# Gathering one more tile in the same batch by plain DMAs, with a Newton root and row copies on VectorE

## The chip, the cores and the metric

One core of a Trainium2 chip runs the whole program. Its engines work side by side, each through a queue of its own: TensorE (PE, with its weight loads as PEld), VectorE (DVE), ScalarE (ACT), GpSimd (POOL) and SyncE (SP, which only issues transfers). The metric is the time of one execution on the device in microseconds (us), taken as the median over runs. One further execution was recorded by the profiler, and all durations below come from it.

## The reference

It is a recommendation network. For a batch of B = 16384 users there are L = 200 history items each; every item id is looked up in a table of 64-number rows, and the rows are weighted by an attention network and summed:

```python
h = i_emb[hist]                       # (200, 16384, 64)
feat = concat([h, it, h - it, h * it])
a = dice(feat @ au_W1 + au_b1, au_alpha, axis=1)
w = a @ au_W2 + au_b2
cur = sum(w * h, axis=0)
# dice(x): p = sigmoid((x - mean) * rsqrt(var + 1e-8)); x * (p + alpha * (1 - p))
```

The mean and variance inside `dice` are taken over the batch, for each history position l by itself. So the attention weights of position l need the statistics of all 16384 rows of l. After the 200 positions a small network of three layers (the head) turns user, item, category and `cur` into two numbers for each user.

## The kernel before

A **tile** is 128 rows of the table, a **step** is 16 tiles (1024 columns of TensorE work once transposed), and a history position l is 8 steps, c = 0 to 7, so that step k = 8l + c. There are 1600 steps. The first 180 positions run in a hardware loop of 45 positions per turn, the last 20 and the head are written out.

Every step is put into the engines' queues by `step` (L383), in the order of its lines, which is kept as written. Step k fetches its own tiles, turns those of step k−1 (transposes on VectorE, matmuls on TensorE), moves the hidden layer of step k−2 out of PSUM, and applies the attention weights to step k−9, whose position has its statistics by then:

- `fetch` (L319): GpSimd issues one indirect DMA for each tile (L123), into one of 5 buffers `rows`. A buffer is free again when the transposes of step k−5 have read it.
- `hidden` (L338): ScalarE copies the PSUM tile `px` to `xs` with the bias added (L339).
- at the end of a position (when k−2 is the last step of l) `measure` and `moments` (L341, L363): VectorE takes the batch statistics of l. `scale_and_shift` (L167) forms 1/sqrt(var + eps) from them: a Sqrt on ScalarE (L170), then a reciprocal and one multiplication on VectorE (L171, L172). Sqrt and Sigmoid need different tables on ScalarE, so each such root brings two table loads with it.
- `gate` (L326): ScalarE takes the sigmoid of `xs` of step k−9 (L328), with scale and shift of its position.
- `place` (L346) and `rows_by_address` (L279): see below.
- `turn` (L354): four transposes on VectorE (L156), then matmuls into `ph` and `px`; `product` (L359): VectorE forms `hm` from `ph` (L360), TensorE adds its part to `px`; `weights` and `weigh` (L330, L334): VectorE forms `y` (L331), TensorE forms `wb`, VectorE multiplies it and adds it to `curT` (L335, L336).

**Tiles by address.** Not all 128 tiles of a position come by indirect DMA. In some steps (c in `SIDES`, that is 1, 3, 4, 5, 6, 7) the 16th tile is fetched row by row, with one plain DMA of 256 bytes for each of its 128 rows. Step c = 5 does so only where l is a multiple of `EACH` = 3, so a position has 6 such tiles in one case of three and 5 otherwise. I call them six-tile and five-tile positions. Their rows are shared evenly over the 8 steps of the position: 96 rows in each step of a six-tile position, 80 in a five-tile one. Half of them are issued by SyncE and half by ScalarE. The addresses are ids times 256, which VectorE scales (L148); an engine reads up to 20 of them into registers with one load (L293) and then issues one DMA for each (L301). The rows land in one of three buffers `side`; each landing counts up a semaphore. In step k+1 `place` waits on ScalarE until all 128 rows have landed, clears the semaphore (`await_rows`, L309), and copies the tile to `rows` on ScalarE (L352). The last tile (c = 7) has its last rows issued in step 7 itself and is placed in step 8, before the next rows are issued.

Where c = 5 is not by address, SyncE loads 128 more ids for it (`sidx`, L142), and GpSimd gathers the 16th tile as the others.

Of the kernel before, what the change touches and what calls it, by code (L numbers as in the profile page):

```python
# [25 lines left out]
SIDES = (1, 3, 4, 5, 6, 7)  # L26
SOMETIMES = 5
EACH = 3
LOAD = 20
ROW = 4 * D  # L30
U8 = mybir.dt.uint8

# [2 lines left out]
def din_kernel(  # L35
# [130 lines left out]

    def scale_and_shift(mean, var, rstd, shift):  # L167
        n = mean.shape[0]
        std = small.tile([P, 1], F32, tag="std", name="std")
        nc.scalar.activation(std[:n], var, AF.Sqrt, bias=eps[:n])  # L170
        nc.vector.reciprocal(rstd, std[:n])  # L171
        nc.vector.scalar_tensor_tensor(shift, mean, -1.0, rstd, ALU.mult, ALU.mult)  # L172

    eps = make("eps", P, 1)
    blk_h = make("blk_h", P, P)
    blk_i = make("blk_i", P, P)
    blk_m = make("blk_m", P, P)
# [9 lines left out]
    halves = [(0, S), (S, A - S)]  # L187

    def attention_weights():
        nc.vector.memset(eps, EPS)  # L190
# [82 lines left out]
    def tiles_by_address(l):  # L273

        round_, i = divmod(l, EACH)
        first = round_ * (EACH * (NS - 1) + 1) + i * (NS - 1) + (i > 0)
        return first, [j for j, c in enumerate(SIDES) if has_side(l * ND + c)]

    def rows_by_address(k):  # L279
        l, s = divmod(k, ND)  # L280
        first, tiles = tiles_by_address(l)
        n = len(tiles) * P // ND // 2
        loads = -(-n // LOAD)
        for i, (engine, issue) in enumerate(
            ((mybir.EngineType.SP, nc.sync), (mybir.EngineType.Activation, nc.scalar))
        ):
            r0, end = (2 * s + i) * n, (2 * s + i + 1) * n
            while r0 < end:
                many = min(end - r0, -(-n // loads))
                at0 = tiles[r0 // P] * P + r0 % P  # L290
                while tiles[(r0 + many - 1) // P] * P + (r0 + many - 1) % P != at0 + many - 1:
                    many -= 1
                _, at = nc.values_load_multi_w_load_instructions(  # L293
                    addr[l % 3][:, at0 : at0 + many],
                    engines=(engine,), min_val=0, max_val=ROW * (V - 1),
                    skip_runtime_bounds_check_because="the DMA checks the address against the table",
                )
                for r, a in enumerate(at, r0):
                    m, p = first + r // P, r % P
                    key = keys.setdefault(m, f"rows{next(serial)}")  # L300
                    dma = issue.dma_start(  # L301
                        side[m % 3].bitcast(U8)[p : p + 1],
                        flat[ds(a, ROW)].rearrange("(o d) -> o d", o=1),
                    ).then_inc(landed[m % 3], 16)
# [78 lines left out]
    def step(k, last=None):  # L383

        def has(j):
            return last is None or j <= last

        ends = (k - 2) % ND == ND - 1
        if has(k):
            fetch(k)  # L390
        if has(k - 2):
            hidden(k - 2)
            if ends:
                measure(k - 2)
                moments((k - 2) // ND)
        if has(k - LAG):
            gate(k - LAG)
        if has(k - 1):
            place(k - 1)
        if has(k):  # L400
            rows_by_address(k)
        if has(k - 1):
            turn(k - 1)
        if has(k - 2) and not ends:
            measure(k - 2)
        if has(k - 1):
            product(k - 1)
        if has(k - LAG):
            weights(k - LAG)
            weigh(k - LAG)  # L410

    def steps(l0, n, end):
        for k in range(n * ND):
            l, c = divmod(k, ND)
            if c == 0 and l + 1 < end:
                load_hist_ids((l + 1) % IDX, l0 + l + 1)
                if (l + 1) % EACH:
# [183 lines left out]
```

## Time and profile before

| | |
|---|---|
| median of 13 runs | 31360.91 us (31251.99 to 31371.98) |
| the profiled execution | 31316.35 us, span 31314.6 us |
| busy: PE / DVE / ACT / POOL | 66% / 48% / 14% / 75% of the span |
| indirect DMAs on GpSimd | 24917, of which 24400 + 133 for the history |
| row DMAs, SyncE and ScalarE | 68288 each |
| granted TensorE clock | 0.805 |

The 13 runs fall into two groups, three near 31252 us and ten near 31360 us; the profiled one lies between them. Busy times count only the work of an engine: the time that ScalarE's queue spends on issuing DMAs, on loads of registers and on waits is not in its 14%. The queue's own rows are marked ACTq and SPq.

### The profile page before, as it was taken

Reading aid. Unit: us, or ns where it says so; the run is one execution under the profiler, and the core shown is the slowest. Engines: PE = TensorE matmul, PEld = TensorE weight load, DVE = VectorE, ACT = ScalarE, POOL = GpSimd, SP = SyncE. Lnnn points to the kernel's source line nnn. Section 1 sums busy time; section 2 is a strip of 40 time slices with the busy share of each in tenths; the row PEclk is TensorE's granted clock in tenths of the full one; section 3 lists DMA queues with packets and bytes.
Section 4 is the critical chain, followed back from the end, with each engine's and each line's share of the span. In section 5 each row is a group of like instructions: output and inputs, shape, how many; then the busy total and the mean of one; then the engine's idle time right before and its main releaser. Section 6 shows DMA issues by size and latency. Waiting matters only on the chain. (4 is left out here: it accounts for less than half of the span.)

```text
span 31314.6 us, 423966 instructions
## 1 busy us (share of the span) xinstructions
PE 20710.0 (66%) x38856; PEld 8498.5 (27%) x38856; DVE 15125.9 (48%) x18955; ACT 4403.8 (14%) x4941; POOL 23586.2 (75%) x24922
## 2 busy tenths in 40 slices
PE   5666666666666666666666666666666666666666
PEld 2222222222222222222222222222222222222222
DVE  4444444444444444444444444444444444444444
ACT  1111111111111111111111111111111111111111
POOL 7777777777777777777777777777777777777776
PEclk7877888887887788888878778888888888878887
DMA  1111111111111111111111111111111111111111
GB/s 29 29 29 29 29 29 29 29 29 29 29 29 29 29 29 29 29 29 29 29 29 29 29 29 29 29 29 29 29 29 29 29 29 29 29 29 29 29 29 24
DMA packets 1130924, 894.71 MB, mean 29 GB/s; under 512 B 729024, under 2 KB 729024, under 8 KB 1127896
## 3 DMA queue, kind: packets, MB, share of 16 engines
q0 software_dynamic: 797344, 818.07, 14.9%
q1 hardware_dynamic: 193112, 31.56, 0.6%
q10 hardware_dynamic: 137440, 17.76, 0.4%
q14 instruction: 2722, 22.30, 0.2%
q8 instruction: 306, 5.01, 0.1%
HBM read 865.10 MB, written 0.13 MB: 28 GB/s over the span
## 5 line engine op out<-in xcount | busy, mean ns | idle before, releaser
L123 POOL DMA_INDIRECT rows<-in_L_rec_i_emb,idx x24400 | 23096.4, 947 | 7472.5 <-issue 7231.1
L161 PE MATMUL ph<-hT,unit 128*128 128x512 f32 x6404 | 5899.2, 1069 | 10403.2 <-DVE hT L156 10401.2
L335 DVE SCALAR_TENSOR_TENSOR wb<-wb,au_bias,hT 128x1024 f32<-128x1024 f32 x1609 | 2080.0, 1293 | 10854.3 <-PE wb L161 10854.3
L156 DVE STREAM_TRANSPOSE hT<-rows 64x512 f32<-64x512 f32 x6404 | 4514.7, 705 | 2687.6 <-ACT rows L352 1797.0
L339 ACT ACTIVATE xs<-px,au_bias 128x1024 f32<-128x1024 f32 x1602 | 1785.1, 1114 | 25635.9 <-issue 11312.0
L161 PEld LDWEIGHTS ph<-hT,unit 128*128 128x128 f32 x6404 | 1727.5, 303 | 13432.7 <-DVE hT L156 13261.7
L161 PE MATMUL px<-hT,blk_h 128*128 128x512 f32 x6404 | 4111.1, 730 | 0.1
L161 PE MATMUL px<-itT,blk_i 128*128 128x512 f32 x6404 | 3342.4, 604 | 0.0
L161 PE MATMUL wb<-y,blk_p 128*128 128x512 f32 x6436 | 3295.2, 594 | 33.3 <-DVE y L331 33.3
L161 PE MATMUL wb<-xs,blk_x 128*128 128x512 f32 x6436 | 3293.2, 593 | 5.3 <-DVE curT L336 5.3
L161 PE MATMUL px<-hm,blk_m 128*128 128x512 f32 x6408 | 3013.0, 592 | 40.7 <-DVE hm L434 40.7
L360 DVE TENSOR_TENSOR hm<-ph,itT 128x1024 f32<-128x1024 f32 x1601 | 1961.1, 1225 | 1908.1 <-PE ph L161 1906.3
L161 PEld LDWEIGHTS px<-hT,blk_h 128*128 128x128 f32 x6404 | 1645.0, 257 | 2411.8 <-issue 2405.0
L344 DVE BATCH_NORM_STATS2 st<-xs 128x6 f32<-128x512 f32 x3204 | 2061.0, 685 | 231.0 <-ACT xs L339 186.0
L336 DVE TENSOR_TENSOR curT<-wb,curT 128x1024 f32<-128x1024 f32 x1609 | 1970.2, 1225 | 54.8
L331 DVE TENSOR_TENSOR y<-pg,xs 128x1024 f32<-128x1024 f32 x1609 | 1954.7, 1215 | 2.3 <-ACT pg L328 2.2
L161 PEld LDWEIGHTS px<-itT,blk_i 128*128 128x128 f32 x6404 | 1394.3, 218 | 2026.4 <-issue 2026.4
L328 ACT ACTIVATE pg<-xs,sh,rs 128x1024 f32<-128x1024 f32 x1609 | 1934.3, 1202 | 25.1 <-DVE y L331 20.1
L161 PEld LDWEIGHTS wb<-y,blk_p 128*128 128x128 f32 x6436 | 1224.9, 190 | 1578.6 <-issue 1539.6
L161 PEld LDWEIGHTS px<-hm,blk_m 128*128 128x128 f32 x6408 | 1217.9, 190 | 1573.4 <-issue 1532.7
L161 PEld LDWEIGHTS wb<-xs,blk_x 128*128 128x128 f32 x6436 | 1223.9, 190 | 1550.9 <-issue 1540.7
L352 ACT COPY rows<-side 128x64 f32<-128x64 f32 x1068 | 249.0, 233 | 315.5 <-DMA side<-in_L_rec_i_emb 179.8
(155 smaller groups left out, 2188.6 us busy)
## 6 DMA issues: line engine op xcount, KB each, us to landing
side<-in_L_rec_i_emb SPq DMA_DIRECT2D x68288, 0.2 KB
side<-in_L_rec_i_emb ACTq DMA_DIRECT2D x68288, 0.2 KB
rows<-in_L_rec_i_emb,idx POOLq DMA_INDIRECT x24400
idx<-in_r_hist SPq DMA_DIRECT2D x200, 61.0 KB
addrs<-in_r_hist SPq DMA_DIRECT2D x200, 3.0 KB
sidx<-in_r_hist SPq DMA_DIRECT2D x133, 0.5 KB
rows<-in_L_rec_i_emb,sidx POOLq DMA_INDIRECT x133
rows<-in_L_rec_i_emb,ids POOLq DMA_INDIRECT x128
```

Of the source, the lines that this page charges most:

```text
L123: nc.gpsimd.indirect_dma_start(out=dst[:, n, :], out_offset=None, in_=table, in_offset=bass.IndirectOffsetOnAxis(ap=ids, axis=0),)
L156: nc.vector.transpose(by_tile(dst[ts(e, D)], i), of[ts(i, D), :, ts(e, S)])
L161: nc.tensor.matmul(dst[:, ts(i, CH)], lhsT, rhs[:, ts(i, CH)], start=(first and j == 0), stop=(last and j == len(pairs) - 1), skip_group_c ...
L328: nc.scalar.activation(pg, xs[k % XR], AF.Sigmoid, bias=shifts[i], scale=rstds[i])
L331: nc.vector.tensor_mul(y, pg, xs[k % XR])
L335: nc.vector.scalar_tensor_tensor(wb, wb, au_bias2, hT[k % LAG], ALU.add, ALU.mult)
L336: nc.vector.tensor_add(curT[k % ND], wb, curT[k % ND])
L339: nc.scalar.activation(xs[k % XR], px, AF.Identity, bias=au_bias)
L344: nc.vector.bn_stats(stats[l % 3][:, 2 * c + i, :], xs[k % XR][:, ts(i, CH)])
L352: nc.scalar.copy(rows[k % ROWS][:, TD - 1], side[m % 3])
L360: nc.vector.tensor_mul(hm, ph, itT[k % ND])
```

## The change

It has four parts.

1. `MOST` = 2: step c = 5 takes its 16th tile by address where l % 3 is 0 or 1, no longer only where it is 0. So two positions of three are six-tile ones.
2. `scale_and_shift` uses no Sqrt. VectorE finds 1/sqrt(v) itself: a first guess by integer arithmetic on the bits, then three Newton steps, 12 small instructions in place of Sqrt and reciprocal.
3. `place` runs on VectorE: it waits there for the rows, clears the semaphore there, and copies the tile.
4. The rows of ScalarE are issued earlier in the step: one run of them (up to 20) between `hidden` and `gate`, the rest after `gate`. SyncE's are issued as before.

```diff
+MOST = 2
 def scale_and_shift(mean, var, rstd, shift):
-        std = small.tile([P, 1], F32, tag="std", name="std")
-        nc.scalar.activation(std[:n], var, AF.Sqrt, bias=eps[:n])
-        nc.vector.reciprocal(rstd, std[:n])
+        nc.vector.tensor_scalar_add(v, var, EPS)
+        nc.vector.tensor_single_scalar(h.bitcast(I32), v.bitcast(I32), 1, ALU.logical_shift_right)
+        nc.vector.tensor_scalar(
+            rstd.bitcast(I32), h.bitcast(I32), -1.0, float(0x5F375A00), ALU.mult, ALU.add
+        )
+        for _ in range(3):
+            nc.vector.scalar_tensor_tensor(h, rstd, v, rstd, ALU.mult, ALU.mult)
+            nc.vector.tensor_scalar(h, h, -0.5, 1.5, ALU.mult, ALU.add)
+            nc.vector.tensor_mul(rstd, rstd, h)
         nc.vector.scalar_tensor_tensor(shift, mean, -1.0, rstd, ALU.mult, ALU.mult)
...
+    def shares(k):
+        l, s = divmod(k, ND)
+        n = len(tiles_by_address(l)[1]) * P // ND
+        many = round(n * SPLIT)
+        runs = []
+        for r0, end in ((s * n, s * n + many), (s * n + many, (s + 1) * n)):
+            loads = -(-(end - r0) // LOAD)
+            at = [r0 + (end - r0) * i // loads for i in range(loads + 1)]
+            runs.append(list(zip(at, at[1:])))
+        return runs
...
     def await_rows(m):
         if m in keys:
-            fence = nc.scalar.wait_ge(landed[m % 3], 16 * P)
+            fence = nc.vector.wait_ge(landed[m % 3], 16 * P)
             tc.declare_fence(fence.ins, group=keys.pop(m))
-            nc.scalar.sem_clear(landed[m % 3])
+            nc.vector.sem_clear(landed[m % 3])
     def has_side(k):
-        return c in SIDES and (c != SOMETIMES or l % EACH == 0)
+        return c in SIDES and (c != SOMETIMES or l % EACH < MOST)
...
             await_rows(m)
-            nc.scalar.copy(rows[k % ROWS][:, TD - 1], side[m % 3])
+            nc.vector.tensor_copy(rows[k % ROWS][:, TD - 1], side[m % 3])
...
+        if has(k):
+            sync, scalar = shares(k)
+            ask(k, 0, sync)
+            ask(k, 1, scalar[:1])
         if has(k - LAG):
             gate(k - LAG)
+        if has(k):
+            ask(k, 1, scalar[1:])
         if has(k - 1):
             place(k - 1)
-        if has(k):
-            rows_by_address(k)
-        if has(k - 1):
             turn(k - 1)
```

`ask` issues one engine's runs as `rows_by_address` did, with one register load for each run of up to 20 rows (`SPLIT` = 0.5, so the halves are as before). The ids of `sidx` are loaded only where c = 5 is not by address.

More of the change, by code (lines that the diff above doesn't have):

```diff
@@ L28 @@
 EACH = 3
+MOST = 2
 LOAD = 20
+SPLIT = 0.5
 ROW = 4 * D
@@ L168, in scale_and_shift @@
         n = mean.shape[0]
-        std = small.tile([P, 1], F32, tag="std", name="std")
-        nc.scalar.activation(std[:n], var, AF.Sqrt, bias=eps[:n])
-        nc.vector.reciprocal(rstd, std[:n])
+        v = small.tile([P, 1], F32, tag="v", name="v")
+        h = small.tile([P, 1], F32, tag="h", name="h")
+        v, h = v[:n], h[:n]
+        nc.vector.tensor_scalar_add(v, var, EPS)
[7 more added lines that the diff above has]
+            nc.vector.tensor_mul(rstd, rstd, h)
         nc.vector.scalar_tensor_tensor(shift, mean, -1.0, rstd, ALU.mult, ALU.mult)
-    eps = make("eps", P, 1)
     blk_h = make("blk_h", P, P)
@@ L189, in attention_weights @@
     def attention_weights():
-        nc.vector.memset(eps, EPS)
         for t in (blk_h, blk_i, blk_m, blk_p, au_bias, au_al, au_w2):
@@ L275, in tiles_by_address, with ask, place_of @@
         round_, i = divmod(l, EACH)
-        first = round_ * (EACH * (NS - 1) + 1) + i * (NS - 1) + (i > 0)
+        first = round_ * (EACH * (NS - 1) + MOST) + i * (NS - 1) + min(i, MOST)
         return first, [j for j, c in enumerate(SIDES) if has_side(l * ND + c)]
-    def rows_by_address(k):
+    queues = ((mybir.EngineType.SP, nc.sync), (mybir.EngineType.Activation, nc.scalar))
+    def shares(k):
         l, s = divmod(k, ND)
-        first, tiles = tiles_by_address(l)
[L282 to L287, printed above, removed]
+        n = len(tiles_by_address(l)[1]) * P // ND
[6 more added lines that the diff above has]
+        return runs
+    def ask(k, queue, runs):
+        l = k // ND
+        first, tiles = tiles_by_address(l)
+        engine, issue = queues[queue]
+        def place_of(r):
+            return tiles[r // P] * P + r % P
+        for r0, end in runs:
             while r0 < end:
-                many = min(end - r0, -(-n // loads))
-                at0 = tiles[r0 // P] * P + r0 % P
-                while tiles[(r0 + many - 1) // P] * P + (r0 + many - 1) % P != at0 + many - 1:
+                many = end - r0
+                while place_of(r0 + many - 1) != place_of(r0) + many - 1:
                     many -= 1
                 _, at = nc.values_load_multi_w_load_instructions(
-                    addr[l % 3][:, at0 : at0 + many],
+                    addr[l % 3][:, place_of(r0) : place_of(r0) + many],
                     engines=(engine,), min_val=0, max_val=ROW * (V - 1),
@@ L416, in steps @@
                 load_hist_ids((l + 1) % IDX, l0 + l + 1)
-                if (l + 1) % EACH:
+                if (l + 1) % EACH >= MOST:
                     load_side_ids((l + 1) % IDX, l0 + l + 1)
```

## Prediction

> **What bounds the kernel now.** I read the groups of the page first, then GpSimd's own timeline, then ScalarE's and VectorE's timelines in the middle of the run, then the list of waits. The groups, and the start and end of GpSimd's timeline:
>
> ```profile
> L123 POOL DMA_INDIRECT rows<-in_L_rec_i_emb,idx x24400 | 23096.4, 947 | 7472.5 <-issue 7231.1
> ```
>
> ```profile
> 2.89 1.09 POOL L123 DMA_INDIRECT rows<-in_L_rec_i_emb,ids  x1 [1.81 <-DMA ids<-in_r_item]
> ...
> 31217.62 0.94 POOL L123 DMA_INDIRECT rows<-in_L_rec_u_emb,ids  x1 [0.30 <-issue]
> ```
>
> GpSimd shows 75% busy, but the rest of its time is "issue", 0.30 us in front of every gather, and no other wait is of any size. With 24917 gathers in the program, the two starts give (31217.62 − 2.89) / 24916 = 1.2528 us for each gather from start to end of the run. GpSimd sets the pace, and the span ends 96 us after its last gather. Three positions hold 122 + 123 + 123 = 368 gathers, so they last 461.0 us, 19.2 us a step.
>
> The second question is how close behind the next engine is. ScalarE is 14% busy, but its queue issues the rows. Its timeline in a stretch from a six-tile position into a five-tile one:
>
> ```profile
> 15023.10 1.11 ACT L339 ACTIVATE xs<-px,au_bias 128x1024 f32<-128x1024 f32 x1 [18.10 <-issue]
> ...
> 15025.51 18.09 ACTq L301 DMA_DIRECT2D side<-in_L_rec_i_emb  x46
> 15043.73 1.11 ACT L339 ACTIVATE xs<-px,au_bias 128x1024 f32<-128x1024 f32 x1 [18.25 <-issue]
> ...
> 15064.57 1.11 ACT L339 ACTIVATE xs<-px,au_bias 128x1024 f32<-128x1024 f32 x1 [18.47 <-issue]
> ...
> 15105.05 1.11 ACT L339 ACTIVATE xs<-px,au_bias 128x1024 f32<-128x1024 f32 x1 [16.09 <-DVE wb L335]
> 15106.18 1.28 ACT L170 ACT_TABLE_LOAD   x1
> 15109.75 0.29 ACT L170 ACTIVATE std<-var,eps 128x1 f32<-128x1 f32 x1 [2.29 <-DVE var L380]
> 15110.07 1.28 ACT L328 ACT_TABLE_LOAD   x1
> 15111.36 1.21 ACT L328 ACTIVATE pg<-xs,sh,rs 128x1024 f32<-128x1024 f32 x1
> 15112.03 14.98 ACTq L301 DMA_DIRECT2D side<-in_L_rec_i_emb  x40
> 15127.12 1.11 ACT L339 ACTIVATE xs<-px,au_bias 128x1024 f32<-128x1024 f32 x1 [14.55 <-DVE wb L335]
> ...
> 15143.93 1.11 ACT L339 ACTIVATE xs<-px,au_bias 128x1024 f32<-128x1024 f32 x1 [14.43 <-PE wb L161]
> ```
>
> The reader should look at the joints: the issuing of one step ends where the next L339 begins (15025.51 + 18.09 = 15043.60, then 15043.73). ScalarE's queue is full. A step with 48 rows of its own takes 20.6 and 20.8 us here, one with 40 rows 16.8 us. GpSimd takes 19.2 us. So ScalarE falls behind in six-tile positions and catches up in five-tile ones. One position costs ScalarE two further things: the root (from 15105.1 to 15111.4, with two table loads of 1.28 us and a wait of 2.3), and the wait for the last tile's rows.
>
> VectorE's loop, from one step's transposes to the next where nothing holds them, is also near:
>
> ```profile
> 15180.80 2.88 DVE L156 STREAM_TRANSPOSE hT<-rows 64x512 f32<-64x512 f32 x4 [0.43 <-DMA rows<-in_L_rec_i_emb,idx]
> ...
> 15197.30 2.87 DVE L156 STREAM_TRANSPOSE hT<-rows 64x512 f32<-64x512 f32 x4
> ```
>
> It takes 16.5 us (17.2 one step earlier), of which some 10 us are waits on TensorE.
>
> **Part 1, the sixth tile.** It removes 67 gathers, one for every l with l % 3 = 1: 67 × 1.2528 = 83.9 us less for GpSimd, and 67 id loads of 0.36 us on SyncE, which nobody waits for. Three positions become 122 + 122 + 123 = 367 gathers or 459.8 us. It adds 67 × 128 = 8576 row DMAs, half on each queue. For ScalarE a five-tile position becomes a six-tile one. The timeline's steps average 20.57 us with 48 rows (20.63, 20.84, and 20.29 and 20.52 in the next six-tile position) and 16.8 with 40 rows, so this adds 8 × 3.77 = 30 us to three positions. SyncE issues 240 rows in 97.22 us, register loads included, 0.405 us each: 1088 rows of three positions cost it 441 us, below 460, so it is no bound.
>
> **Part 2, Newton.** ScalarE loses the root: 6.3 us from L339 to the end of the second table load, of which about 5.7 us held the row issuing behind them. That is 3 × 5.7 = 17 us in three positions. VectorE gets 12 small instructions for one. The moments show such instructions start 0.08 to 0.22 us apart; with 0.18, nearest to the dependent ones (15253.34, .53, .72), it is 12 × 0.18 = 2.2 us (ends 1.0 and 2.6). The waits list has 500.5 us on the line "ACT std L170 <- DVE var L380", which goes altogether.
>
> **Part 3, placing on VectorE.** ScalarE loses the copy, which lay beside its issuing anyway, and the waits for rows. The copy of the last tile of a position comes 2.9 us after the last row issue (15085.81 to 15088.72), so 3 × 2.9 = 9 us go from ScalarE's queue; the remaining waits and clears I take as 0.1 us a step, 2.5 us in three positions. VectorE gets 17 copies in three positions. Before has no 128x64 copy on VectorE: a 32x2 copy takes 0.16 us there, the 128x64 copy on ScalarE 0.23; I take 0.2 (about 3.4 us in three positions; ends 2.7 and 4). The new wait stands in front of the transposes, and behind it in VectorE's queue is the whole step: hm, y, both updates and, at the end of a position, the moments that ScalarE's gate waits for.
>
> At this place a rule speaks against the change. VectorE already does 804 small f32 copies (L370), and the gathers beside them at 15252.37 and 15253.61 still take 0.94 us with 0.30 between. The Trainium skill, page "SBUF — State Buffer", section with the box on the "DVE blocks DMA" trap, says that an f32 copy from SBUF to SBUF on VectorE keeps GpSimd from writing descriptors, and gives 620 ns growing to 3100 ns for a DMA issued there. By the page, 1134 copies that each hold a gather by 2.48 us would add 2812 us; by the row, nothing. I take the row.
>
> **Part 4, rows between x and gate.** It adds no work. It hides the time until the new root is ready: L339 to var is 4.65 us (15105.05 to about 15109.7), plus 2.2 and 0.2 for the shift, 7.1 us. The first run of rows lasts 16 / 48 of 20 us, 6.7, or half of 16.4, 8.2 us. So the gate waits 0 to 1 us, unless VectorE begins its moments late.
>
> **The sum.** ScalarE's queue without any wait, for three positions: two six-tile ones 2 × 8 × (20.57 − 0.1) = 327.5, one five-tile one 8 × (16.8 − 0.1) = 133.6, together 461.1 us. The same count for before is 8 × 20.57 + 16 × 16.8 + 3 × (5.7 + 2.9) = 459.2, which agrees with an engine that just keeps up with 461.0. So GpSimd's 459.8 is no longer what decides. To 461.1 come waits of the new order. In a five-tile position VectorE needs 8 × 16.8 + 5 × 0.2 + about 6.2 (statistics 1.3, moments 2.4, Newton 2.2, shift 0.2) = 141.6 us against ScalarE's 133.6. Of these 8 us I let 3 be absorbed by the distance between the two queues: 5 us. Where a six-tile position follows, the gate waits about 0.2 to 0.5 us, twice: 0.5 us. So three positions take about 466.5 us instead of 461.0, and 200 positions 66.7 × 5.5 = 367 us more. Once, some 55 us of this are swallowed: GpSimd is ahead by up to five buffers (5 × 19.2 = 96 us, less one step for filling and 5 to 28 us of distance to the transposes, 49 to 72 us), and the head lets the others catch up while GpSimd gathers its 256 tiles. The profiled execution would go from 31316 to about 31628. The median of before lies 45 us above the profiled execution, its lower group 64 below; with half of the 45 I say 31650.
>
> **Rivals.**
> - *The pace stays with GpSimd.* It needs ScalarE to manage three positions in 459.8 us, that is 6.7 us less than I count. The mean of a row with its register load, 0.42 us, would have to be 1.5% smaller, or the waits nearly nil. For it: I estimate from a handful of steps. Against: the joints above show no spare time at all. Time: 31361 − 84 = 31277, the full gain.
> - *Even.* Three positions in about 460.9 to 462.8 us, where the 55 us of buffers eat the loss: 31300 to 31420.
> - *VectorE becomes the pace in every position.* It now waits for the last rows of a position (2.9 us after ScalarE's last issue), and then does moments and Newton in one queue. If nothing of this is absorbed, a five-tile position gives 8 us and each six-tile position about 2 us of waits: 461.1 + 12 = 473, 66.7 × 12 − 55 = 745 us more, about 32080. For it: VectorE holds all three chains. Against: a six-tile step leaves VectorE 20.5 − 16.8 = 3.7 us, so 8 steps absorb it.
>
> **How the numbers follow.** Likeliest, ScalarE's queue sets the pace with 463 to 470 us: 0.55. VectorE in every position: 0.15. Even: 0.08. GpSimd still: 0.22. A difference under 0.2%, 63 us, can't be told from none in this kernel. Faster 0.22, same 0.08, slower 0.70. The likeliest alone gives 31420 to 31900. The range for 8 in 10 goes down to GpSimd's case, 31260, and up to 32000.
>
> **What would show it.** 24850 gathers. If I am right, GpSimd has idle time that is released by "DVE hT L156" (full buffers) instead of issue alone, growing over the run; ScalarE's steps with 48 rows still take 20.4 us without gaps; no Sqrt and no table load in the loop; in five-tile positions L339 waits on PE. If GpSimd's starts stay 1.253 us apart to the end, the first rival holds. If VectorE's transposes wait mostly on "DMA side", or VectorE's loop is above 18 us, the third does. I would be wrong above all if a row's issue cost changed: 1% of it is 4 us in three positions, 270 us in all.

## The result, and the profile after

The changed kernel takes 31956.65 us (median of 8 runs, 31953.28 to 31965.15), the kernel before beside it 31358.76. The ratio is 1.0194, with a 95% interval of 1.0184 to 1.0204. So the change makes the kernel 1.9% slower. The forecast had the direction and about half of the size: 31650, with 32000 as the upper end. The profiled execution of after has a span of 31979.1 us (before: 31314.6) and a granted TensorE clock of 0.788 (before: 0.805). One remark on the numbers of the experiments: in e1 to e4 and e11 to e16 the kernel before itself takes 50980 to 51436 us, and from one row to the next on ScalarE's queue some 0.6 us pass on the mean instead of 0.34, for a reason that no run shows, so these runs are no evidence on the change.

First GpSimd, which paced the kernel before. From the groups of the page of after; the columns are line, engine, operation and tiles, then busy time and mean ns of one, then idle time before it and what ended most of it:

```profile
L125 POOL DMA_INDIRECT rows<-in_L_rec_i_emb,idx x24400 | 23101.6, 947 | 8199.1 <-issue 7187.4
...
L375 DVE COPY rows<-side 128x64 f32<-128x64 f32 x1135 | 244.5, 215 | 1283.8 <-DMA side<-in_L_rec_i_emb 1274.0
```

A gather still takes 947 ns. But 8199.1 us of idle time stand before the gathers instead of 7472.5, and not all of it is issue any more. The waits list of after has the new entries (total us, times, longest):

```profile
POOL rows L125 <- issue: 7320.8, 23961, 0.3
...
DVE rows L375 <- DMA side<-in_L_rec_i_emb: 1274.0, 146, 13.3
...
POOL rows L125 <- DVE hT L158: 543.5, 148, 7.6
...
POOL rows L125 <- DVE rows L375: 196.0, 35, 62.2
```

GpSimd is now held by "DVE hT L158": it has filled its five buffers and waits for the transposes to empty one. By their starts, 512 of these 543.5 us lie in five-tile positions. (Of the 196.0 us on the last line, 186 are three waits of 62 us between two turns of the hardware loop.) The pace has gone to the engines behind GpSimd. VectorE's new wait for the rows ("DMA side") has 146 entries, 134 of them at the end of a six-tile position, as will be seen.

To see where, I take the starts of `hidden` (L339 before, L362 after) at the same step of every position, over the middle of the run:

| mean of a position | before | after | predicted |
|---|---|---|---|
| l % 3 = 0 | 170.0 (six tiles) | 162.3 (six) | 163.7 (six) |
| l % 3 = 1 | 144.6 (five) | 164.4 (six) | 163.7 (six) |
| l % 3 = 2 | 146.4 (five) | 144.7 (five) | 138.6 (five) |
| three | 461.0 | 471.4 | 466.5, with 0.5 for the gate |

The six-tile positions are as predicted, 163.35 us on the mean, and the whole miss lies in the five-tile position. The windows view of after shows three positions one by one (window, its us, then busy us of PE, PEld, DVE, ACT and POOL with counts, granted clock, DMA share, GB/s):

```profile
9595.10:9757.30 162.20, 106.95 (x194) 41.86 (x192) 80.25 (x112) 18.58 (x17) 122.81 (x130) 0.79 0.16 29
9757.30:9922.30 165.00, 108.27 (x192) 42.68 (x192) 78.04 (x110) 18.60 (x17) 123.75 (x132) 0.76 0.16 28
9922.30:10066.10 143.80, 102.73 (x191) 42.57 (x192) 74.38 (x107) 18.55 (x16) 100.64 (x107) 0.79 0.15 27
```

In the third row GpSimd issues only 107 gathers in 143.8 us, where it could do 114 (143.8 / 1.2528): this is the stretch where it is held. ScalarE's timeline across the joint from six to five tiles shows what does it:

```profile
9909.07 13.10 ACTq L324 DMA_DIRECT2D side<-in_L_rec_i_emb  x32
9922.27 1.11 ACT L362 ACTIVATE xs<-px,au_bias 128x1024 f32<-128x1024 f32 x1 [13.40 <-issue]
...
9932.34 6.34 ACTq L324 DMA_DIRECT2D side<-in_L_rec_i_emb  x20
9939.67 1.11 ACT L362 ACTIVATE xs<-px,au_bias 128x1024 f32<-128x1024 f32 x1 [7.76 <-PE wb L163]
...
9950.77 6.83 ACTq L324 DMA_DIRECT2D side<-in_L_rec_i_emb  x20
9963.35 1.11 ACT L362 ACTIVATE xs<-px,au_bias 128x1024 f32<-128x1024 f32 x1 [12.93 <-PE wb L163]
...
9972.96 6.42 ACTq L324 DMA_DIRECT2D side<-in_L_rec_i_emb  x20
9980.64 1.11 ACT L362 ACTIVATE xs<-px,au_bias 128x1024 f32<-128x1024 f32 x1 [8.12 <-PE wb L163]
```

Up to 9922 the issuing ends where L362 begins (9909.07 + 13.10 = 9922.17): the queue is full, as in a six-tile step before. From there on it has holes. The rows issued from 9950.77 end at 9957.60, and L362 comes 5.75 us later, released by TensorE; the rows from 9972.96 end at 9979.38, and the hole is 1.26 us. Over the positions 30 to 149 the time from the last row of a step to L362 adds up to 11.9 us in a five-tile position, and to 1.2 and 1.3 us in the two six-tile ones. ScalarE now waits for the recurrent chain over TensorE and VectorE.

### The profile page after: what moved, and what is told of

It is laid out like the page before. It is cut to its first block, busy times and chain, and to the rows that moved or that the text cites. A ratio compares the mean times of both kernels' runs of the same rounds, so it can differ in the third digit from the quotient of the medians.

```text
span 31979.1 us, 443348 instructions
## 1 busy us (share of the span) xinstructions
PE 21305.4 (67%) x38856; PEld 8508.2 (27%) x38856; DVE 15730.1 (49%) x22333; ACT 3788.2 (12%) x3263; POOL 23528.0 (74%) x24855
## 5 line engine op out<-in xcount | busy, mean ns | idle before, releaser
L125 POOL DMA_INDIRECT rows<-in_L_rec_i_emb,idx x24400 | 23101.6, 947 | 8199.1 <-issue 7187.4
L163 PE MATMUL px<-hT,blk_h 128*128 128x512 f32 x6404 | 4349.2, 769 | 480.7 <-ACT xs L362 480.1
L158 DVE STREAM_TRANSPOSE hT<-rows 64x512 f32<-64x512 f32 x6404 | 4517.2, 705 | 222.5 <-DMA rows<-in_L_rec_i_emb,idx 58.0
L362 ACT ACTIVATE xs<-px,au_bias 128x1024 f32<-128x1024 f32 x1602 | 1785.4, 1115 | 17886.8 <-PE wb L163 6354.1
L163 PE MATMUL px<-itT,blk_i 128*128 128x512 f32 x6404 | 3552.9, 638 | 0.0
L163 PEld LDWEIGHTS px<-itT,blk_i 128*128 128x128 f32 x6404 | 1460.8, 228 | 2125.0 <-issue 2125.0
L375 DVE COPY rows<-side 128x64 f32<-128x64 f32 x1135 | 244.5, 215 | 1283.8 <-DMA side<-in_L_rec_i_emb 1274.0
```

Of the source, the lines that this page charges most:

```text
L125: nc.gpsimd.indirect_dma_start(out=dst[:, n, :], out_offset=None, in_=table, in_offset=bass.IndirectOffsetOnAxis(ap=ids, axis=0),)
L158: nc.vector.transpose(by_tile(dst[ts(e, D)], i), of[ts(i, D), :, ts(e, S)])
L163: nc.tensor.matmul(dst[:, ts(i, CH)], lhsT, rhs[:, ts(i, CH)], start=(first and j == 0), stop=(last and j == len(pairs) - 1), skip_group_c ...
L362: nc.scalar.activation(xs[k % XR], px, AF.Identity, bias=au_bias)
```

## The experiments

My theory (A) after the result: in five-tile positions VectorE's loop with TensorE sets the pace, with nothing absorbed; in six-tile positions the queues that issue the rows do. The rivals: VectorE's new work and waits are the loss, part 3 above all (B), the copies keep GpSimd from writing descriptors (C), ScalarE's issuing is the bound in five-tile positions as well (D), VectorE is the bound everywhere (E). The new order of rows and gate (part 4) has no run of its own.

### Parts 2 to 4 without part 1, and part 1 without parts 2 to 4

```diff
-MOST = 2
+MOST = 1
```

> The changed kernel with c = 5 by address in one position of three again, so parts 2 to 4 without part 1. Theory A (ScalarE's row issuing paces six-tile positions with 163.5 us, the loop of VectorE and TensorE paces five-tile ones with about 144.7 us, whoever is slowest over three positions decides): 163.5 + 2 x 144.7 = 453 us, under GpSimd's 461.0, so GpSimd paces and the time is that of before, 31250 to 31420 us. Rival B (the loss comes from VectorE's new work and waits, part 3 above all): VectorE keeps its 1067 copies, the waits for rows and Newton, so most of the loss stays, 31650 to 31950 us. Rival C (the copies keep GpSimd from writing descriptors): the gap between gathers grows over 1.253 us, and the time with it.

> Parts 2 to 4 without part 1 once more, since on the chip of the first four runs the kernel before itself took 51382 us. Theory A (six-tile positions paced by ScalarE's issuing with 163.5 us, five-tile ones by the loop of VectorE and TensorE with about 144.7 us): 163.5 + 2 x 144.7 = 453 us in three positions, under GpSimd's 461.0, so GpSimd paces: the time of before, 31250 to 31420 us. Rival B (VectorE's new work and waits are the loss): 31650 to 31950 us. Rival C (the copies keep GpSimd from writing descriptors): gathers more than 1.253 us apart.

e1: 51473.4 against 51381.72 us. e5: 31321.24 us against 31346.48, ratio 0.9989, interval 0.9978 to 1.0. GpSimd's group in the page of e5:

```profile
L125 POOL DMA_INDIRECT rows<-in_L_rec_i_emb,idx x24400 | 23039.6, 944 | 7467.9 <-issue 7180.9
```

The idle time is back at 7467.9 us, and a gather takes 944 ns beside the copies on VectorE. So C is out as a reason for the loss. Parts 2 to 4 alone slow nothing either, but here GpSimd sets the pace again, and by A's count (453 us against 461 in three positions) up to 8 us of a cost of parts 2 to 4 could hide behind it. The reverse run closes this gap for B.

It is the kernel before with part 1 alone:

```diff
+MOST = 2
-        first = round_ * (EACH * (NS - 1) + 1) + i * (NS - 1) + (i > 0)
+        first = round_ * (EACH * (NS - 1) + MOST) + i * (NS - 1) + min(i, MOST)
-        return c in SIDES and (c != SOMETIMES or l % EACH == 0)
+        return c in SIDES and (c != SOMETIMES or l % EACH < MOST)
-                if (l + 1) % EACH:
+                if (l + 1) % EACH >= MOST:
```

> The kernel before with c = 5 by address in two positions of three, root, place and order of rows as before, so part 1 alone. Theory A: ScalarE's own steps of before take 170.0 us in a six-tile position and 145.5 in a five-tile one (both with root and row wait), so three positions take 2 x 170 + 146 = 486 us instead of 461: 66.7 x 25 = 1670 us more, less some 50 us of buffers, about 32950 us (32700 to 33200). Rival B: without the new work on VectorE the 67 gathers fewer are a gain, 31277 us.

> Part 1 alone on the kernel before, once more on a chip where that takes 31360 us. Theory A: with root and place still on ScalarE's queue a six-tile position takes it 170.0 us and a five-tile one 145.5, 486 us for three against GpSimd's 459.8: 66.7 x 25 = 1670 us more than before, 32700 to 33200 us. Rival B (part 3 is the loss): 31277 us.

e2: 52962.1 us, ratio 1.0315. e10: 32984.24 us, ratio 1.0549, interval 1.0529 to 1.0569. Positions take 171.2, 171.3 and 144.3 us. So the loss comes from part 1, and B is out for parts 2 to 4 together: once the sixth tile is in two of three positions, parts 2 to 4 are worth 32984 − 31957 = 1027 us, or 15.4 us in three positions: some 8 us in each six-tile position and nothing in the five-tile one, which has 144.3 us without them and 144.7 with them.

### Fewer rows for ScalarE, more for SyncE, in six-tile positions

e3 gives SyncE 50 of the 96 rows and ScalarE 46; e4 does the same with two register loads in place of three (`LOAD` = 25).

```diff
-        many = round(n * SPLIT)
+        many = {96: 50, 80: 40}[n]
```

> The changed kernel with 50 of the 96 rows of a step on SyncE and 46 on ScalarE in six-tile positions, five-tile ones left at 40 and 40. Theory A: ScalarE's six-tile position falls by 8 x 2 x 0.336 = 5.4 us, twice in three positions, 471.1 - 10.8 = 460.3: 66.7 x 10.8 = 720 us less than the changed kernel, about 31240 to 31350 us, if SyncE keeps up (it has 50 rows x 0.327 + 3 loads x 1.35 = 20.4 us a step there, 16.8 in five-tile positions, 459 us in three). Rival B: VectorE's chain is untouched, so 31900 to 31960 us. If SyncE can't keep up: VectorE's waits for rows grow and the time is 31500 to 31900.

> As the run with 50 and 46 rows, and up to 25 addresses are read by one register load in place of 20, so that a step of a six-tile position has two loads on each queue instead of three. A load of 16 addresses takes 1.33 us and one of 20 takes 1.48, so one of 23 should take about 1.6: ScalarE's six-tile step becomes 46 x 0.336 + 2 x 1.6 + 0.2 = 18.9 us. Theory A: three positions are 2 x 151 + 144.7 = 447 us for ScalarE, so GpSimd paces with 459.8: the full gain of 84 us over before, 31230 to 31290 us. Rival B: 31900 us, as VectorE's work is the same.

55715.94 and 55811.87 us, 1.085 and 1.087 times the kernel before beside them. Both are misses. The loads of 15 and of 23 addresses that came with the edit take 3.44 and 5.13 us on ScalarE (see the next experiment), so these runs tell nothing about the share of rows.

### Fewer rows for ScalarE in five-tile positions

e6 gives SyncE 42 and ScalarE 38 of the 80 rows.

```diff
-        many = round(n * SPLIT)
+        many = {96: 48, 80: 42}[n]
```

> The changed kernel with 42 of the 80 rows of a step on SyncE and 38 on ScalarE in five-tile positions alone; six-tile ones stay at 48 and 48. ScalarE's step there has two rows less, 0.75 us with the shorter loads, 6 us in the position. Theory A: five-tile positions follow the loop of VectorE and TensorE, so nothing changes, 31900 to 31990 us. Rival D (ScalarE's issuing paces five-tile positions too): three positions fall by 6 us, 66.7 x 6 = 400 us, 31500 to 31620 us. SyncE has 42 x 0.327 + 3 x 1.3 = 17.6 us a step there, 141 us in the position, and 160 in a six-tile one, 461 in three, under the 471 that the changed kernel takes.

33548.12 us, ratio 1.0693, interval 1.0661 to 1.0725. Far outside all that I had written. ScalarE's 38 rows go in two runs of 19, and the register loads in front of these (L316), in a five-tile position of e6, durations in ns as min/median/max:

```profile
L316 SPq TENSOR_LOAD <-addrs x9: 1421/1433/3202, 9929.7 to 9982.7; - x9
L316 ACTq TENSOR_LOAD <-addrs x5: 4218/4294/4363, 9931.7 to 9974.6; - x5
```

A load of 19 addresses takes 4.3 us on ScalarE, where one of 20 takes 1.44. Two of these a step add 5.7 us, more than the two rows taken away save. The edit had a second effect larger than the first.

e8 avoids this with sizes that divide by four: SyncE 24 + 20, ScalarE 20 + 16.

```diff
-        many = round(n * SPLIT)
-        runs = []
-        for r0, end in ((s * n, s * n + many), (s * n + many, (s + 1) * n)):
-            loads = -(-(end - r0) // LOAD)
-            at = [r0 + (end - r0) * i // loads for i in range(loads + 1)]
+        runs, r0 = [], s * n
+        for sizes in {96: ((16, 16, 16), (16, 16, 16)), 80: ((24, 20), (20, 16))}[n]:
+            at = [r0]
+            for size in sizes:
+                at.append(at[-1] + size)
+            r0 = at[-1]
```

> The changed kernel with 44 of the 80 rows of a step on SyncE (loads of 24 and 20) and 36 on ScalarE (20 and 16) in five-tile positions; six-tile ones as they are. ScalarE's step there has four rows and 0.2 us of loads less, 1.5 us, 12 us in the position; all counts are multiples of four, unlike the 19 of the earlier run. Theory A: five-tile positions follow the loop of VectorE and TensorE (144.7 us), so the time stays within 31880 to 31990 us. Rival D (ScalarE's issuing paces them too): 66.7 x 10 to 12 us less, 31160 to 31290 us, with GpSimd as the floor.

32004.27 us, ratio 1.0236, interval 1.022 to 1.0253. ScalarE's timeline in a five-tile position of e8 (its L363 is L362 of after):

```profile
9931.67 5.37 ACTq L325 DMA_DIRECT2D side<-in_L_rec_i_emb  x16
9939.67 1.11 ACT L363 ACTIVATE xs<-px,au_bias 128x1024 f32<-128x1024 f32 x1 [8.21 <-PE wb L163]
...
9972.82 5.45 ACTq L325 DMA_DIRECT2D side<-in_L_rec_i_emb  x16
9980.43 1.11 ACT L363 ACTIVATE xs<-px,au_bias 128x1024 f32<-128x1024 f32 x1 [7.82 <-PE wb L163]
```

ScalarE has 36 rows instead of 40 here and L363 starts at the same time as in after (9939.67 in both). The hole in front of it grew from 0.99 to 2.63 us. The five-tile position takes 144.4 us, in after 144.7 by the same mean. ScalarE got 1.6 us back in this step, and the position did not shorten by it. So D is out: the rows do not set the pace there.

### An addition on VectorE, in five-tile and in six-tile positions

Both add work that the reference does not have, one 128x1024 addition on VectorE a step behind `weigh`; e9 in five-tile positions, e17 in six-tile ones (e11, e13 and e15 are the same kernel as e17). e18 is the changed kernel itself beside e17.

```diff
+        if has(k) and k // ND % EACH == MOST:     # e9;  e17: < MOST
+            nc.vector.tensor_add(ucT[3], ucT[3], ucT[3])
```

> The changed kernel with one more 128x1024 addition on VectorE at the end of every step of five-tile positions alone (1.23 us, on a scratch tile). Theory A: VectorE's loop paces these positions, so 8 x 1.3 us more in three positions, 66.7 x 10.4 = 690 us: 32500 to 32750 us. Rival D (ScalarE paces them, VectorE has time left): 31950 to 32050 us.

32327.36 us, ratio 1.0339; 371 us over the changed kernel, where I had expected 540 to 790. The additions are 528 times 1.218 us, 643 us in all. The five-tile position goes from 144.7 to 149.1. Its windows row:

```profile
10045.90:10194.70 148.80, 98.95 (x191) 41.41 (x192) 82.67 (x114) 18.58 (x16) 102.91 (x107) 0.83 0.14 26
```

VectorE has 8 us more to do (82.67 instead of 74.38), the position is 5 us longer, and TensorE is busy 3.8 us less for the same work, at a granted clock of 0.83 instead of 0.79. So the addition does lie on the path, as A says. The size was off: of 9.7 us that eight additions take, 4.4 arrive. TensorE's shorter time makes up most of the rest (2.9 us on the mean over the positions, 102.4 to 99.5); what remains is not explained.

> The changed kernel with one more 128x1024 addition on VectorE (1.23 us, on a scratch tile) at the end of every step of six-tile positions alone, the counterpart of the run with the addition in five-tile ones, which cost 370 us. Theory A (in six-tile positions the queues that issue rows set the pace, 20.4 us a step, and VectorE's loop of 17.1 us has 3.3 us to spare): nothing but up to 1.2 us later moments at two ends of positions, 31950 to 32130 us. Rival E (VectorE's loop is the pace everywhere): 66.7 x 16 x 1.23 us = 1310 us more, or half of it if TensorE runs faster in the longer pauses, 32600 to 33270 us.

> The addition on VectorE in six-tile positions alone (1.23 us a step) once more, on a chip where the kernel before takes 31360 us. Theory A (the queues that issue rows set the pace there, 20.4 us a step, and VectorE's loop of 17.1 us has 3.3 us to spare): up to 1.2 us later moments at two ends of positions, 31950 to 32130 us. Rival E (VectorE's loop is the pace everywhere): 66.7 x 16 x 1.23 us = 1310 us more, or half of it if TensorE runs faster in the longer pauses, 32600 to 33270 us.

> The addition on VectorE in six-tile positions alone (1.23 us a step), a third time for a chip where the kernel before takes 31360 us. Theory A (the queues that issue rows set the pace there, 20.4 us a step, and VectorE's loop of 17.1 us has 3.3 us to spare): up to 1.2 us later moments at two ends of positions, 31950 to 32130 us. Rival E (VectorE's loop is the pace everywhere): 1310 us more, or half of it if TensorE runs faster in the longer pauses, 32600 to 33270 us.

> The addition on VectorE in six-tile positions alone (1.23 us a step). Where the kernel before takes 31360 us: theory A (the queues that issue rows set the pace there, VectorE has 3.3 us to spare) 31950 to 32130 us; rival E (VectorE's loop is the pace everywhere) 32600 to 33270 us. On a chip like that of the last three calls: the same ratio to before as the unchanged change of this call, within 0.3%, by theory A.

> The changed kernel as it is, as the control of this call. Where the kernel before takes 31360 us it takes 31957. On a chip like that of the last three calls, theory A and rival E agree on nothing that was measured; I estimate 1.02 to 1.03 of before from the runs there, since 6% more rows go through queues that are the bound for every kernel there: the addition in six-tile positions had 1.028 to 1.030, part 3 undone 1.031 to 1.034.

e11, e13 and e15 took 1.0279, 1.0301 and 1.0276 times the kernel before: inconclusive, with no changed kernel beside them. e17's two runs took 31863.16 and 31904.79 us, e18's two 31945.28 and 31958.31. VectorE does 1072 additions more, 1304 us, and the kernel is not slower but some 68 us faster (medians 31883.98 and 31951.79). ScalarE's timeline in a six-tile position of e17:

```profile
9639.52 12.07 ACTq L324 DMA_DIRECT2D side<-in_L_rec_i_emb  x32
9651.69 1.11 ACT L362 ACTIVATE xs<-px,au_bias 128x1024 f32<-128x1024 f32 x1 [12.37 <-DVE wb L358]
9653.04 5.11 ACTq L324 DMA_DIRECT2D side<-in_L_rec_i_emb  x16
9658.20 1.21 ACT L351 ACTIVATE pg<-xs,sh,rs 128x1024 f32<-128x1024 f32 x1 [5.39 <-issue]
9659.60 12.18 ACTq L324 DMA_DIRECT2D side<-in_L_rec_i_emb  x32
9671.88 1.11 ACT L362 ACTIVATE xs<-px,au_bias 128x1024 f32<-128x1024 f32 x1 [12.47 <-DVE rows L375]
```

The queue is still full: 9639.52 + 12.07 = 9651.59, then L362; a step is 20.2 us. Six-tile positions take 162.4 and 164.3 us, in e18 162.4 and 164.7. Even with the additions, VectorE's last step of a six-tile position, the one with the wait for the rows, lasts 28 us on the mean (29 to 30 in after), where a step with an addition and no such wait needs some 18. So E is out: there VectorE has time to spare, and the issuing paces.

The additions had a side effect on GpSimd:

```profile
L125 POOL DMA_INDIRECT rows<-in_L_rec_i_emb,idx x24400 | 23502.1, 963 | 7733.8 <-issue 7218.6
```

Its gathers take 963 ns on the mean instead of 947. In the trace 904 gathers last more than 1 us, up to 2.00, and 882 of these overlap such an addition; after has 96, up to 1.32 us, each beside the scaling of the addresses (L150). GpSimd is busy 400 us longer by this, and the kernel still isn't slower: GpSimd does not set its pace.

### Two register loads of 24 in place of three of 16

```diff
-LOAD = 20
+LOAD = 24
```

> The changed kernel with up to 24 addresses in a register load, so that the 48 rows of a six-tile step take two loads of 24 on each queue in place of three of 16. The changed kernel's loads take 0.55 us for 4 addresses, 1.27 for 16 and 1.44 for 20; going on like this 24 take about 1.6 (the 19 of the last run took 4.3, so a count may also be a bad one). Theory A: ScalarE's six-tile step falls by 3 x 1.3 - 2 x 1.6 = 0.7 us, 11 us in three positions, 471.1 - 11 = 460: GpSimd and ScalarE level, 31220 to 31340 us, at or just under the kernel before. Rival B (VectorE's new work and waits): 31900 us. A bad count: 4 us more a step, 34000 us and over.

31791.78 us, ratio 1.0168, interval 1.0154 to 1.0183: 165 us better than the changed kernel, where I had expected 31220 to 31340. A six-tile step has two loads of 1.73 us in place of three of 1.27, and these positions go from 162.3 and 164.4 to 159.2 and 159.5. But the five-tile position goes from 144.7 to 150.0, though VectorE's loop in it is as long as before: its eight steps from transposes to transposes add up to 143.9 us, in after to 143.8. What grew is the wait in front of it. VectorE's timeline at its start in e7:

```profile
9848.89 1.23 DVE L359 TENSOR_TENSOR curT<-wb,curT 128x1024 f32<-128x1024 f32 x1
9862.03 0.20 DVE L375 COPY rows<-side 128x64 f32<-128x64 f32 x1 [11.92 <-DMA side<-in_L_rec_i_emb]
```

and ScalarE's at the same place:

```profile
9844.04 7.93 ACTq L324 DMA_DIRECT2D side<-in_L_rec_i_emb  x24
9852.08 1.11 ACT L362 ACTIVATE xs<-px,au_bias 128x1024 f32<-128x1024 f32 x1 [8.71 <-issue]
9861.70 6.56 ACTq L324 DMA_DIRECT2D side<-in_L_rec_i_emb  x20
9875.91 1.11 ACT L362 ACTIVATE xs<-px,au_bias 128x1024 f32<-128x1024 f32 x1 [14.63 <-PE wb L163]
```

The last row of the six-tile position is issued by 9851.97, and VectorE has its tile only at 9862.03, 10 us later; in after the copy came 3.3 us after the last issue (9922.17 to 9925.49). At this joint it is 9.7 us on the mean in e7 and 4.0 in after; SyncE's share of the rows has been issued some 40 us before it in both. The DMA queues tell why. 60 us in front of the joint, e7 (9790 to 9850; queue, then packets, MB, and the time of their packets as a share of 16 engines; then the issues):

```profile
q1 hardware_dynamic: 420, 0.10, 4.2%
q10 hardware_dynamic: 281, 0.04, 4.2%
...
side<-in_L_rec_i_emb ACTq DMA_DIRECT2D x150, 0.2 KB
side<-in_L_rec_i_emb SPq DMA_DIRECT2D x149, 0.2 KB
```

and after, 9860 to 9920:

```profile
q1 hardware_dynamic: 428, 0.10, 0.8%
q10 hardware_dynamic: 276, 0.04, 0.4%
...
side<-in_L_rec_i_emb SPq DMA_DIRECT2D x142, 0.2 KB
side<-in_L_rec_i_emb ACTq DMA_DIRECT2D x139, 0.2 KB
```

As many packets in q10, which carries ScalarE's rows, take 4.2% of 16 × 60 us in e7, 143 ns each, and 0.4% in after, 14 ns. By the packets' starts, a row of ScalarE starts 0.7 us after its issue in after. In e7 this grows through the two six-tile positions to 5.1 us in the last step (7.3 for the latest twentieth), and is back at 0.8 by the third step of the five-tile one. In these two stretches the transfers do not keep up with 299 rows in 60 us, and do with 281. e7 also issues its rows in runs of 24 instead of 16; no run separates the rate from the longer runs. So some 5 of the 8 us that ScalarE's queue gave back in three positions went into late rows.

### Placing on ScalarE again (part 3 undone)

`await_rows`, the clear and the copy are on ScalarE, ahead of the asks.

```diff
-            fence = nc.vector.wait_ge(landed[m % 3], 16 * P)
+            fence = nc.scalar.wait_ge(landed[m % 3], 16 * P)
-            nc.vector.sem_clear(landed[m % 3])
+            nc.scalar.sem_clear(landed[m % 3])
-            nc.vector.tensor_copy(rows[k % ROWS][:, TD - 1], side[m % 3])
+            nc.scalar.copy(rows[k % ROWS][:, TD - 1], side[m % 3])
```

> The changed kernel with part 3 undone: wait, clear and copy of the placed tiles on ScalarE again, ahead of the step's rows; root and order of the rows stay. Theory A: ScalarE's queue gets back the wait for the last rows, 2.9 us at the end of a position, and some 0.17 us for each tile; in the two six-tile positions that is 2 x 3.9 = 8 us on the pace, in the five-tile one VectorE's loop hides it: 66.7 x 6 to 8 us more, 32300 to 32550 us. Rival B (the waits and copies on VectorE are what the change loses by): less than the changed kernel, 31300 to 31700 us.

> Part 3 undone (wait, clear and copy of the placed tiles on ScalarE, ahead of the step's rows) once more, on a chip where the kernel before takes 31360 us. Theory A: 2 x 3.9 = 8 us more on ScalarE's queue in the two six-tile positions, in the five-tile one VectorE's loop hides it: 32300 to 32550 us. Rival B (the waits and copies on VectorE are the loss): less than the changed kernel, 31300 to 31700 us.

> Part 3 undone (wait, clear and copy of the placed tiles on ScalarE, ahead of the step's rows), a third time for a chip where the kernel before takes 31360 us. Theory A: 2 x 3.9 = 8 us more on ScalarE's queue in the two six-tile positions, in the five-tile one VectorE's loop hides it: 32300 to 32550 us. Rival B (the waits and copies on VectorE are the loss): less than the changed kernel, 31300 to 31700 us.

52590.42, 53187.85 and 52631.93 us, 1.0314, 1.0338 and 1.0322 times the kernel before, each 0.3 to 0.5% above the kernel with the addition (e11, e13, e15) beside it. That says nothing sure about the change. What part 3 is worth alone stays open.

No kernel of these beats the kernel before: e5 is level with it, and all with six tiles in two positions are slower.

## Why the prediction was right and wrong

**The balance of the span.** From the first `hidden` to the last:

```profile
205.27 1.11 ACT L362 ACTIVATE xs<-px,au_bias 128x1024 f32<-128x1024 f32 x1 [12.31 <-PE wb L163]
...
31635.72 1.11 ACT L362 ACTIVATE xs<-px,au_bias 128x1024 f32<-128x1024 f32 x1 [12.16 <-PE wb L163]
```

These are 31430.4 us in after and 30710.8 in before (214.9 to 30925.7), 719.6 more, or 10.8 us for each three positions. The start in front is 9.6 us shorter, and the tail behind 45.5 us shorter (343.4 instead of 388.9), because GpSimd arrives there ahead: its last gather starts 241.3 us after the last `hidden` instead of 291.9. 719.6 − 9.6 − 45.5 = 664.5, the difference of the spans. So "Once, some 55 us of this are swallowed" came out in its sum, 9.6 + 45.5 = 55.1, but partly by luck: the 45.5 us are what it described, a little below its 49 to 72, and the 9.6 us at the start are nothing it spoke of. The term of 5.5 us in three positions did not come out: it measured 10.8 (10.4 by the table above, over the middle of the run), and (10.8 − 5.5) × 66.6 = 353 us is the whole miss against the 31628 forecast for the profiled execution, which took 31980.9.

**The step that failed** is "Of these 8 us I let 3 be absorbed by the distance between the two queues: 5 us", the term of the five-tile position: it was put at 133.6 + 5 = 138.6 us and measured 144.7. Two things were off. First, nothing is absorbed: the position takes 144.7 us, and VectorE's loop from transposes to transposes adds up to 143.8 there (mean of positions 30 to 149), with no wait for rows inside it. The distance gave nothing; between the two counts 0.9 us were even lost, which no run explains. As I now read the rows, the two queues could not lie far apart there: ScalarE's L362 waits for TensorE's products, these for VectorE's transposes, and VectorE's update for ScalarE's gate, all in the same few steps. The distance that I thought would absorb it is used up in the first step: VectorE comes into the five-tile position waiting for the last rows. VectorE's timeline of after:

```profile
9914.40 1.23 DVE L359 TENSOR_TENSOR curT<-wb,curT 128x1024 f32<-128x1024 f32 x1
9925.49 0.20 DVE L375 COPY rows<-side 128x64 f32<-128x64 f32 x1 [9.87 <-DMA side<-in_L_rec_i_emb]
9925.92 2.88 DVE L158 STREAM_TRANSPOSE hT<-rows 64x512 f32<-64x512 f32 x4 [0.23 <-DVE rows L375]
...
9946.54 0.15 DVE L175 TENSOR_SCALAR v<-var 128x1 f32<-128x1 f32 x1
...
9949.02 0.16 DVE L184 SCALAR_TENSOR_TENSOR sh<-mean,rs 128x1 f32<-128x1 f32 x1
9949.39 2.88 DVE L158 STREAM_TRANSPOSE hT<-rows 64x512 f32<-64x512 f32 x4 [0.21 <-issue]
...
9966.68 0.18 DVE L375 COPY rows<-side 128x64 f32<-128x64 f32 x1
9966.90 2.88 DVE L158 STREAM_TRANSPOSE hT<-rows 64x512 f32<-64x512 f32 x4
...
9981.50 1.29 DVE L358 SCALAR_TENSOR_TENSOR wb<-wb,au_bias,hT 128x1024 f32<-128x1024 f32 x1 [6.95 <-PE wb L163]
...
9983.97 2.87 DVE L158 STREAM_TRANSPOSE hT<-rows 64x512 f32<-64x512 f32 x4
...
10069.67 2.88 DVE L158 STREAM_TRANSPOSE hT<-rows 64x512 f32<-64x512 f32 x4
```

After the first line the copies wait for nothing, and what VectorE waits for is TensorE ("PE wb"). Here the loop takes 10069.67 − 9925.92 = 143.75 us.

Second, the loop itself is 143.8 us on the mean and not 141.6. The step with the moments takes 23.5 us, where my terms (16.8 + 6.2) give 23.0; the other seven take 120.3, 17.2 each, where 7 × 16.8 and the five copies give 118.6. Of these 2.2 us, 0.55 is the scaling of the addresses (L150), which I forgot. The rest I put to TensorE's lower clock, and that is argued, not shown: the granted clock is 0.79 on the mean of these positions and 0.82 in five-tile positions of before, but TensorE's busy time differs by only 0.7 us (102.4 and 101.7). So of the 6.1 us that the position lies above 138.6, 3 are the absorption that did not come, 2.2 the loop, and 0.9 the loss between the queues.

**The six-tile position** was right: 163.7 predicted, 163.35 measured, and e17 shows that it is the issuing and not VectorE that takes this time. The gate's 0.5 us cannot be told apart in that.

**SyncE** was called no bound from its mean over three positions (441 us). In a six-tile position that is too friendly. It issues 288 rows, six steps, in 118.03 us, 19.7 a step, against ScalarE's 20.4. Its last rows of a six-tile position are still issued some 38 us before the copy that waits for them, ScalarE's 4 us. So it is no bound for this change, but it stands 4% behind ScalarE.

**The smaller costs.** Newton from the end of the variance to the shift: 9946.54 to 9949.02, 2.48 us with its twelve instructions, predicted 2.2. The copy: 215 ns, predicted 0.2. The gathers beside 1135 such copies: 947 ns and 0.30 us between, as before. 928 of the 1134 copies that wait for rows start while a gather runs, and the only gathers over 1 us among those are the 96 beside the scaling of the addresses. The Trainium skill (page "SBUF — State Buffer", section "SBUF: two separate sides" with the box on the "DVE blocks DMA" trap) says that such copies keep GpSimd from writing descriptors; my estimate from its figures, 3100 − 620 ns for each copy, was 2812 us. This trace does not show it, and the row was the right choice. The wait for the variance is gone, as said, and of 416 table loads 10 are left, 8 of them where a turn of the hardware loop ends. Parts 2 to 4 save some 8 us in each six-tile position by e10, where I had 5.7 for the root, 2.9 for the last copy and 0.8 for the waits of eight steps, 9.4 in all.

**The rivals.** GpSimd staying the pace was nearer than it looks. ScalarE's 133.6 us for the five-tile position agree with the trace (144.7 less 11.9 of holes, of which 0.1 a step stand in a full queue too); with the position at that, three would have taken 162.3 + 164.4 + 133.6 = 460.3 us, beside GpSimd's 459.8. What kept it out is the five-tile position alone, and my argument against it, that the joints in six-tile positions are tight, was not the one that decided. "VectorE in every position" came nearest in time (32080), and half of it is what happened: nothing is absorbed in the five-tile position. Its other half, 2 us in each six-tile position, is refuted by their 163.35 us and by e17.

## What to carry to other kernels

A mean over stages hides which queue is the bound in each: count each stage's own pace, the slowest engine of each, and add those up; a slower stage is only made up for by a faster one if something between them can hold the lead. Here, as I read the rows, the two queues wait for each other within a few steps, so nothing could, and the longest loop counts in full. When an engine's issuing is shortened, look next at whether the transfers it starts can still keep up.

## What the runs showed of the hardware

- **A register load's time goes by more than its size.** On ScalarE 4 addresses take 0.55 us, 16 take 1.27, 20 take 1.44 and 24 take 1.73; but 3 take 0.96 (e6), 15 take 3.44 (e3), 19 take 4.30 (e6) and 23 take 5.13 (e4). All the cheap ones divide by four. On SyncE 14, 17 and 25 addresses took 1.43 (e6), 1.52 (e3) and 2.07 (e4), beside 1.23 for 16, 1.45 for 20 and 1.68 for 24, without that jump. Why the two queues differ was not tested.
- **Row transfers can run late at little more than the rate at which they are prompt.** With gathers of GpSimd beside them, 281 rows in 60 us from both queues start 0.7 us after their issue with some 14 ns for a packet (after); 299 rows in 60 us, in runs of 24, run up a delay of 5 us and 143 ns for a packet (e7).
- **An added wait can raise TensorE's granted clock, but waiting does not fix it.** The addition on VectorE raised it from 0.79 to 0.83 in five-tile positions (e9), with 2.9 us less of busy time for the same matmuls, and from 0.790 to 0.814 over the whole run when put into six-tile positions (e17), where the kernel became slightly faster with more work. But the six-tile positions of e7 are 3 to 5 us shorter than in after, so TensorE stands idle some 2 us less in them, and they have 0.82 and 0.81 where after has 0.79 and 0.78.
- **Which VectorE instructions delay a gather.** Copies of 128x64 did not (947 ns with them, as without). Additions of 128x1024 with both operands in SBUF (the memory that the tiles of rows lie in, not PSUM) did: in e17 882 of the 904 gathers over 1 us, up to 2.00 us long, overlap one. The additions to `curT`, of the same size but with one operand in PSUM, did not (953 ns on the mean for the longest gather beside one, in after).
